# A chain of convolutions and a Haar shrinkage: every matrix product on four 64x64 tiles of the array, images in blocks of 64 rows

## The chip, the cores and the metric

The kernel runs on one core of a Trainium2 chip. Its time is the device time of one execution, in microseconds (us). Each measurement is the median of several executions; the profile comes from one execution of its own. The engines are named as in the profile: PE multiplies matrices (PEld is its loading of weights), DVE is the vector engine, ACT the scalar engine, POOL the general one, and SP issues the DMAs.

## The reference, cut to what matters

The input is `x` with 4 images of 64 channels, 256x256 each, all in float32. Four layers follow each other:

```python
x = conv(x, filters of layer 0)      # L0
x = shrink(x, v, conv_w, tau)        # L1
x = conv(x, filters of layer 2)      # L2
x = conv(x, filters of layer 3)      # L3
```

A convolution layer makes two one-dimensional filters of 256 values for each channel (`hx`, `hy`, small networks of sines), and convolves each image with their product, causally in both directions:

```python
k = jnp.einsum('ijk,imk->ijmk', hx, hy)[0]           # by channel: outer product
y = irfft2(rfft2(x, s=(512, 512)) * rfft2(k, s=(512, 512)) / 512)[..., :256, :256]
out = y + x * bias[:, None, None]
```

The shrinkage layer transforms each image with a two-dimensional Haar transform, and mixes the channels twice:

```python
f1 = haar2d(x)
for i in range(2):
    f4 = jnp.einsum('bchw,oc->bohw', f1 * v[i], conv_w[i])
    acc = acc + jnp.sign(f4) * relu(jnp.abs(f4) - tau[i])
out = haar2d(acc, inverse=True) + x
```

A separable causal convolution is a product with a triangular Toeplitz matrix on each side, so the kernel computes it with matrix products: first one side ("rows"), which also turns the image, then the other ("columns"), which turns it back.

## The kernel before, in words

**Phases.** A round `t` holds two channels of two images, 4 images of 256x256. There are 32 rounds for each of two groups (pairs of batch entries), 64 in all. Phase A does layer 0 and the forward Haar transform, and stores coefficients in DRAM (`coef`). Phase B takes coefficients of all 64 channels, mixes and shrinks them and stores them (`mixed`), in 64 steps of two units for each group. Phase C does the inverse Haar transform and layers 2 and 3, and stores the result.

**Order.** The schedule is written out by hand. Each phase is a list of small pieces; `beside(main, side, ...)` runs a main list and spreads a side list evenly between its pieces. The stages in time are: A for group 0 alone, with the making of the filters beside it; A for group 1 with B for group 0 beside it, called B(0); a short passage from the last of A to the first of C; C for group 0 with B(1) beside it; C for group 1 alone. Each engine works its instructions in the order of the program. `later` keeps back the reading of a PSUM bank until the next piece begins (`flush`).

**Toeplitz products.** `toeplitz` (L282 to L287) is called for each image and each side. An image lies on all 128 partitions, as two blocks of 128 rows. For each of two column blocks it issues a matmul with 256 columns (L286) and one with 128 (L287), since the upper triangle is zero:

```python
nc.tensor.matmul(ps[:, m, :], data[:, 0, cut], t[:, which, :], start=True, stop=False)
nc.tensor.matmul(ps[:, m, HALF:], data[:, 1, cut], t[:, which, :HALF], start=False, stop=True)
```

That is one bank of PSUM per image; four banks (`acps`) rotate. ACT copies the bank of a row product to SBUF (L363 in A, L774 in C); DVE adds `bias` times the old image to that of a column product (L374, L788). `load_toeplitz` (L121) loads the Toeplitz matrices of two channels from DRAM, four DMAs of 128 KB.

**Haar transforms.** One direction is done along the free axis by POOL (`forward_free`, L295/L300, 16 operations in A; `inverse_free`, L321/L323, 16 in C). The other is on PE in several forms: A multiplies with a Haar matrix of 128 (L394, copied out by ACT at L403), or, for half the images of its first 30 rounds, transposes (L412) and lets DVE do the sums (L434 to L464). C multiplies one half and transposes the other (L717, L718), with ACT and DVE putting them together (L727, L724, L725); its last 32 rounds transpose only (L739), with 17 sums on DVE (L750 to L760) for each half of a round. `coarsest` (L467) has three small POOL operations per round.

**Phase B.** One unit multiplies coefficients with weights of `conv_w` (`mix`), multiplies the result by `v` (L579, DVE), takes its sign (L588, ACT) and its magnitude (L591, ACT), subtracts `tau` (L595, DVE), and shrinks (L598, DVE). POOL adds the results (`add`, L603/L606; packed: L617/L620). B(0) is unpacked: rows of 64 channels and two neighbouring image rows lie on the partitions, and a unit is two matmuls of the whole array with 512 columns (L575). B(1) is packed: a unit is four matmuls on 64x64 tiles (L564), whose results lie crossed, so ACT copies half of them to the other half of the partitions (`exchange`, L613). B(0) loads `v` and `tau` (L550) as two rows of 4 KB, repeated for 64 channels; B(1) loads them from copies in DRAM (`v2`, `taus2`), 16 rows with 8 repeats each.

**DMAs.** All are issued by SP in order. A round of A loads `x` (1 MB), and stores its coefficients in one DMA (L479, 1 MB); a round of C loads `g` in one (L695) and stores `out` in one (L797). A step of B loads `ft`, `v` and `tau` and stores `mixed`, 512 KB each.

## Time and profile before

| | us |
|---|---|
| median of 3 executions | 2809.62 (2809.46 to 2810.77) |
| the profiled execution | 2810.75 |
| its span, first to last instruction | 2809.0 |
| busy PE, DVE, POOL, ACT | 2763.1, 1964.7, 1955.6, 1275.8 |
| 384 Toeplitz passes: L286 with L287 in each of the six products of a round | 309 + 197 busy for each of six |
| A alone, about 34 rounds | 24 to 484 |
| A with B(0) | 484 to 1119 |
| the passage | 1119 to 1163 |
| C with B(1), 30 rounds | 1163 to 2015 |
| C alone, 34 rounds | 2015 to 2809 |

The stages are told apart by the first and last instruction of L575 and L564. Busy times of a group are unions: two records of one matmul overlap, and groups overlap each other, so those of L286 and L287 don't add up to PE's. A float32 matmul leaves two records of its own and two weight loads. The granted clock of PE is full (1.00) throughout. 661.91 MB are moved at a mean of 236 GB/s.

### The profile page before, as it was taken

What the parts mean: (1) busy time and instruction counts of PE and PEld (TensorE: products, weight loads), DVE (VectorE), ACT (ScalarE), POOL (GpSimd) and SP (SyncE); (2) the same over time, 40 slices, a digit from 0 to 9 for tenths busy, and PEclk for the clock granted to TensorE, in tenths of its full rate; (3) what the DMA queues carried; (4) which work ended last, traced back from release to release, by engine and by line L of the source; (5) the groups of instructions that cost most, each with busy time, mean ns of one, the idle gap of its engine ahead of it and who ended that gap; (6) DMA issues with size and microseconds to landing.
All of it is one profiled execution on the core that took longest, in us unless ns stands there. A gap on an engine that the chain in (4) does not pass through costs nothing.

```text
span 2809.0 us, 47062 instructions
## 1 busy us (share of the span) xinstructions
PE 2763.1 (98%) x16940; PEld 2343.8 (83%) x16940; DVE 1964.7 (70%) x3461; ACT 1275.8 (45%) x1859; POOL 1955.6 (70%) x2486
## 2 busy tenths in 40 slices
PE   7999999999999999999999999999999999999999
PEld 6989999777777777877777787777899999999998
DVE  3676663888878888378888888888755566666664
ACT  2344443555555555366666666666522222222222
POOL 3777777888888889867777777777764445555540
PEclk9999999999999999999999999999999999999999
DMA  7758886988888887599989989999644444444442
GB/s 205 231 186 263 260 258 248 345 323 320 324 323 320 324 322 277 197 291 287 276 261 267 280 270 277 270 263 281 188 155 144 148 137 139 137 137 135 136 139 80
DMA packets 237447, 661.91 MB, mean 236 GB/s; under 512 B 26622, under 2 KB 135711, under 8 KB 204704
## 3 DMA queue, kind: packets, MB, share of 16 engines
q1 hardware_dynamic: 237216, 658.90, 72.0%
q8 instruction: 136, 2.23, 0.3%
q14 instruction: 95, 0.78, 0.1%
HBM read 438.60 MB, written 220.20 MB: 235 GB/s over the span
## 4 chain that ended last, share of the span: by engine, by line
PE 86%; DVE 5%; issue 3%; POOL 2%; ACT 2%; DMA 1%; SPq 0%; DVEq 0%; ACTq 0%; POOLq 0%
PE c2c L286 8%; PE c1r L286 8%; PE c1c L286 8%; PE c2r L286 8%; PE a1ps L286 6%; PE f L575 6%; PE a2ps L286 6%; PE f L564 5%; PE c2c L287 4%; PE c1c L287 4%; PE c2r L287 4%; PE c1r L287 4%; PE a3ps L394 4%; PE a1ps L287 3%; PE a2ps L287 3%
## 5 line engine op out<-in xcount | busy, mean ns | idle before, releaser
L588 ACT ACTIVATE m<-f 128x1024 f32<-128x1024 f32 x256 | 262.3, 1024 | 495.5 <-DVE f L579 468.2
L595 DVE TENSOR_TENSOR f<-f,tau 128x1024 f32<-128x1024 f32 x256 | 315.0, 1230 | 164.0 <-ACT f L591 163.8
L579 DVE TENSOR_TENSOR f<-f,v 128x1024 f32<-128x1024 f32 x256 | 314.4, 1228 | 57.7 <-PE f L564 38.9
L286 PE MATMUL a1ps<-toep,x 128*128 128x256 f32 x1024 | 308.3, 383 | 3.2 <-DMA toep<-filt 3.2
L598 DVE SCALAR_TENSOR_TENSOR m<-f,m 128x1024 f32<-128x1024 f32 x256 | 311.1, 1215 | 0.0
L286 PE MATMUL c2c<-toep,ch 128*128 128x256 f32 x1024 | 309.2, 384 | 0.0
L286 PE MATMUL c1c<-toep,ch 128*128 128x256 f32 x1024 | 309.1, 384 | 0.0
L286 PE MATMUL c2r<-toep,cy 128*128 128x256 f32 x1024 | 309.1, 384 | 0.0
L286 PE MATMUL a2ps<-toep,ay 128*128 128x256 f32 x1024 | 305.7, 380 | 0.0
L774 ACT COPY ch<-c2r 128x512 f32<-128x512 f32 x256 | 149.4, 586 | 329.0 <-PE c2r L287 328.3
L774 ACT COPY ch<-c1r 128x512 f32<-128x512 f32 x256 | 148.7, 586 | 314.7 <-PE c1r L287 314.2
L617 POOL TENSOR_TENSOR gt<-m,ft 128x1024 f32<-128x1024 f32 x64 | 151.4, 2365 | 180.2 <-DVE m L598 180.1
L575 PE MATMUL f<-ft,mix 128*128 128x512 f32 x512 | 248.4, 608 | 18.4 <-DVE m L598 11.2
L591 ACT ACTIVATE f<-f 128x1024 f32<-128x1024 f32 x256 | 263.0, 1027 | 0.0
L374 DVE SCALAR_TENSOR_TENSOR x<-x,bias_sb,a2ps 128x512 f32<-128x512 f32 x256 | 188.1, 742 | 69.5 <-PE a2ps L287 59.7
L321 POOL TENSOR_TENSOR i<-g 128x8 f32<-128x8 f32 x63 | 13.6, 216 | 320.3 <-DMA g<-mixed 320.2
L788 DVE SCALAR_TENSOR_TENSOR o<-cy,bias_sb,c2c 128x512 f32<-128x512 f32 x256 | 188.6, 742 | 65.7 <-PE c2c L287 58.4
L403 ACT ACTIVATE f<-a3ps,wcol_sb 128x512 f32<-128x512 f32 x196 | 130.7, 686 | 217.8 <-PE a3ps L394 206.6
L321 POOL TENSOR_TENSOR i<-i,g 128x16 f32<-128x16 f32 x378 | 206.1, 545 | 25.9
L287 PEld LDWEIGHTS a1ps<-toep,x 128*128 128x128 f32 x1024 | 195.9, 191 | 27.0
L287 PEld LDWEIGHTS a2ps<-toep,ay 128*128 128x128 f32 x1024 | 194.6, 190 | 26.4
L287 PEld LDWEIGHTS c1c<-toep,ch 128*128 128x128 f32 x1024 | 194.6, 190 | 26.3
(102 smaller groups left out, 6957.2 us busy)
## 6 DMA issues: line engine op xcount, KB each, us to landing
toep<-filt SPq DMA_DIRECT2D x768, 128.0 KB, 4.1
coef<-f SPq DMA_DIRECT2D x64, 1024.0 KB, 4.4
ft<-coef SPq DMA_DIRECT2D x128, 512.0 KB, 7.1
v<-in_v SPq DMA_DIRECT2D x128, 512.0 KB, 8.0
tau<-taus SPq DMA_DIRECT2D x128, 512.0 KB, 7.6
mixed<-gt SPq DMA_DIRECT2D x128, 512.0 KB, 5.4
g<-mixed SPq DMA_DIRECT2D x64, 1024.0 KB, 7.9
x<-in_x SPq DMA_DIRECT2D x63, 1024.0 KB, 8.4
```

Source lines behind the costliest of these rows:

```text
L286: nc.tensor.matmul(ps[:, m, :], data[:, 0, cut], t[:, which, :], start=True, stop=False)
L287: nc.tensor.matmul(ps[:, m, HALF:], data[:, 1, cut], t[:, which, :HALF], start=False, stop=True)
L321: engine.tensor_tensor(even, s, d, ALU.add)
L374: lambda: nc.vector.scalar_tensor_tensor(s["x1"][:, cut], s["x"][:, cut], bias_sb[:, c : c + 1], ps, ALU.mult, ALU.add)
L575: nc.tensor.matmul(un[u]["f4"][:, j, :], mixers[0][:, u % 2, :], f[:, j, :], start=True, stop=True)
L579: nc.vector.tensor_tensor(f4, f4, weights(u, "v"), ALU.mult)
L588: nc.scalar.activation(un[u]["m"], un[u]["f4"], AF.Sign)
L591: nc.scalar.activation(un[u]["f4"], un[u]["f4"], AF.Abs)
L595: nc.vector.tensor_tensor(f4, f4, weights(u, "tau"), ALU.subtract)
L598: nc.vector.scalar_tensor_tensor(un[u]["m"], un[u]["f4"], 0.0, un[u]["m"], ALU.max, ALU.mult)
L774: later(lambda: nc.scalar.copy(y, ps))
L788: later(lambda: nc.vector.scalar_tensor_tensor(o, old, bias_sb[:, at : at + 1], ps, ALU.mult, ALU.add))
```

## The change

All images are kept as four blocks of 64 rows, and two images of a round lie on the lower half of the partitions, two on the upper. Each product is a set of 64x64 matmuls, and each set goes round the four tiles (row half r, column half c) of the array. A Toeplitz product has four row blocks j, each with four accumulating steps of 256, 192, 128 and 64 columns; a call fills one half of a pair of banks for all four images, and the pair is copied out after two calls.

The Haar transform of the second direction is a set of 64x64 matmuls too, in A (`haar`) and in C, for all rounds; transposes and sums on DVE are gone. POOL's forward transform stops at four sums, and `coarsest` makes the rest, in five operations; two of the coarsest combinations are left to phase B, which does them once for its first two steps (`join`, `part`). B is packed for both groups. A's columns, products and stores run one round later each against its rows, and C does the second convolution of a round beside the first of the next. Coefficients lie in DRAM by step, so that a step reads and writes whole runs, and a round stores and loads them in four DMAs. `x` and `out` are laid out in DRAM as the kernel reads and writes them. B(0) is spread over 27.5 rounds of A, which it joins at 34.5; B(1) over 30 of C.

The diff, cut to its core:

```diff
-PERIOD = N + P
-REPEATS = 24
+PERIOD = N + ROW
+REPEATS = 20
...
+    coef = [coefficients(f"coef{g}") for g in range(GROUPS)]
+    mixed = [coefficients(f"mixed{g}") for g in range(GROUPS)]
...
+    def banks(name):
+
+        return [acps.tile([P, 2, N], F32, tag="ps", name=f"{name}_{r}") for r in range(2)]
...
+    def load_toeplitz(l, t):
...
+        tx = ac.tile([P, CI, N], F32, tag="tx", name=f"tx{l}_{t}", bufs=5)
+        ty = ac.tile([P, N], F32, tag="ty", name=f"ty{l}_{t}", bufs=5)
...
+        for e in range(CI):
+            for r in range(2):
+                rows(tx[r * ROW : (r + 1) * ROW, e, :], 0, e)
+        for e in range(CI):
+            rows(ty[e * ROW : (e + 1) * ROW, :], 1, e)
...
-    def toeplitz(ps, data, t, which):
-
-        for m in range(2):
-            cut = bass.ts(m, P)
-            nc.tensor.matmul(ps[:, m, :], data[:, 0, cut], t[:, which, :], start=True, stop=False)
-            nc.tensor.matmul(ps[:, m, HALF:], data[:, 1, cut], t[:, which, :HALF], start=False, stop=True)
+    TILES = [(r, c) for r in range(2) for c in range(2)]
...
+    def toeplitz(ps, data, t, j):
+
+        for k in range(BLOCKS):
+            for r, c in TILES:
+                nc.tensor.matmul(
+                    ps[r][half(c), j % 2, k * ROW :],
+                    data[half(r), c, k, bass.ts(j, ROW)],
+                    t(r, c)[:, : N - k * ROW],
+                    start=k == 0,
+                    stop=k == BLOCKS - 1,
+                    tile_position=(r * ROW, c * ROW),
+                )
+
+    def haar(ps, data, matrix, j):
+
+        for k in range(BLOCKS):
+            for r, c in TILES:
+                nc.tensor.matmul(
+                    ps[r][half(c), j % 2, bass.ts(k, ROW)],
+                    data[half(r), c, k, bass.ts(j, ROW)],
+                    matrix[half(r)],
+                    start=True,
+                    stop=True,
+                    tile_position=(r * ROW, c * ROW),
+                )
...
     def forward_free(src, dst, name):
 
         cur, half = src, HALF
-        while half >= 1:
+        while half >= BLOCKS:
...
+    def all_rows(grp_tile, c0, images):
+
+        parts = images.rearrange("p (s n) k -> p s (n k)", s=2)
+        return [(rows_of(grp_tile, c0 + e, bp), parts[half(e), bp]) for e in range(CI) for bp in range(2)]
...
+        def product(t, bp):
...
+            two = banks(f"a3ps{bp}_{t}")
+            for j in (2 * bp, 2 * bp + 1):
+                haar(two, blocks(s["fw"]), haarH_sb, j)
+            for b, ps in enumerate(two):
+                f = s["f"][:, 4 * bp + 2 * b : 4 * bp + 2 * b + 2]
+                copy = nc.vector.tensor_copy if b and t < ROUNDS else nc.scalar.copy
+                later(lambda f=f, ps=ps, copy=copy: copy(f, ps))
...
+            nc.gpsimd.tensor_tensor(sums, pair[:, :, :, 0], pair[:, :, :, 1], ALU.add)
+            nc.gpsimd.tensor_tensor(diffs, pair[:, :, :, 0], pair[:, :, :, 1], ALU.subtract)
+            nc.gpsimd.tensor_tensor(f[:, :, 0], sums[:, :, 0], sums[:, :, 1], ALU.add)
+            nc.gpsimd.tensor_tensor(f[:, :, 1], sums[:, :, 0], sums[:, :, 1], ALU.subtract)
+            nc.gpsimd.tensor_tensor(f[:, :, 2:4], diffs, diffs, ALU.add)
...
+            for to, f in all_rows(coef[grp], c0, st[t]["f"]):
+                nc.sync.dma_start(to, f)
...
+            if j < BLOCKS:
+                if t < total:
+                    rows(t, j)
+                if t > 1:
+                    run(st[t - 2]["ops"], 3)
+                if j == 1 and t > 2:
+                    coarsest(t - 3)
+            elif j < 2 * BLOCKS:
+                if 0 < t <= total:
+                    columns(t - 1, j - BLOCKS)
+                if j == BLOCKS and t > 2:
+                    store(t - 3)
+            else:
+                if t > 1:
+                    product(t - 2, j - 2 * BLOCKS)
+                if 0 < t <= total:
                     run(st[t - 1]["ops"], 2)
...
+                at = src.offset + s * 4 * W * COPIES
+                flat = bass.AP(src.tensor, at, [[2 * W, 2 * COPIES], [0, C // COPIES], [1, 2 * W]])
...
+        def join():
+
+            a, b, c, d, t, u = four("f")
+            op = nc.vector.tensor_tensor
+            op(t, a, b, ALU.add)
+            op(b, a, b, ALU.subtract)
+            op(u, c, d, ALU.add)
+            op(d, c, d, ALU.subtract)
+            nc.vector.tensor_copy(c, b)
+            op(a, t, u, ALU.add)
+            op(b, t, u, ALU.subtract)
...
+        def part():
+
+            a, b, c, d, t, u = four("g")
+            op = nc.gpsimd.tensor_tensor
+            op(t, a, b, ALU.add)
...
+            if j < BLOCKS:
+                if t < total:
+                    rows(t, 1, j)
+            elif j < 2 * BLOCKS:
+                if t > 0:
+                    rows(t - 1, 2, j - BLOCKS)
+            elif j < 2 * BLOCKS + 2:
+                product(t + 1, j - 2 * BLOCKS)
+            elif j < 3 * BLOCKS + 2:
+                if t < total:
+                    columns(t, 1, j - 2 * BLOCKS - 2)
+            elif t > 0:
+                columns(t - 1, 2, j - 3 * BLOCKS - 2)
...
+    cut_a, cut_c = (ROUNDS + 2) * A_PIECES + BLOCKS + 1, (ROUNDS - 2) * C_PIECES
+    beside(a[:cut_a], rest, 2, 3 * A_PIECES)
...
+    beside(a[cut_a : -2 * A_PIECES], phase_b(0), 2, 0)
...
+    beside(main, phase_b(1), len(c_first) + 2 * BLOCKS + 6, 0)
```

## The prediction

> **What bounds the kernel now.** I read the busy times first, then the stretches between the stages (busy us and instruction count of PE, weight loads, DVE, ACT, POOL; granted clock; DMA share; GB/s).
>
> ```profile
> PE 2763.1 (98%) x16940; PEld 2343.8 (83%) x16940; DVE 1964.7 (70%) x3461; ACT 1275.8 (45%) x1859; POOL 1955.6 (70%) x2486
> ```
>
> ```profile
> 24.00:484.00 460.00, 457.41 (x3025) 426.79 (x3025) 272.82 (x676) 184.45 (x333) 341.85 (x628) 1.00 0.76 240
> 484.00:1119.00 635.00, 616.61 (x3112) 461.58 (x3111) 512.99 (x488) 363.20 (x472) 558.84 (x642) 1.00 0.88 323
> 1119.00:1163.00 44.00, 41.66 (x290) 39.00 (x289) 21.17 (x38) 17.09 (x28) 34.21 (x59) 1.00 0.51 186
> 1163.00:2015.00 852.00, 850.18 (x5497) 680.52 (x5495) 680.13 (x848) 537.80 (x735) 633.98 (x622) 1.00 0.90 269
> 2015.00:2809.00 794.00, 790.21 (x5015) 732.52 (x5008) 467.79 (x1388) 170.71 (x292) 385.79 (x533) 1.00 0.41 134
> ```
>
> The stages are A alone, A with B(0), the passage, C with B(1), C alone. PE is full in all; beside B, POOL and DMA are next. A busy PE need not be PE at its peak, so next the timeline, where starts count and ends are modelled.
>
> ```profile
> 1500.56 0.60 PE L286 MATMUL c2r<-toep,cy 128*128 128x256 f32 x2
> 1500.99 0.38 PE L287 MATMUL c2r<-toep,cy 128*128 128x128 f32 x2
> 1501.21 0.60 PE L286 MATMUL c2r<-toep,cy 128*128 128x256 f32 x2
> ```
>
> A product leaves two records. Two of 256 columns take 0.43 us, two of 128 take 0.22: PE streams without gaps, loads are hidden. The sum: 384 passes (64 rounds x 6) x 8 x 0.655 = 2012 us; unpacked mixing 512 x 0.429 = 220; packed 128 x 1.02 = 131; L394 1568 x 0.112 = 175; transposes and L717 1520 x 0.111 = 168. That is 2706 of 2763 busy.
>
> Then four tiles, where the kernel already uses them (L564):
>
> ```profile
> 1503.93 1.09 PE L564 MATMUL f<-ft,mix 64*64 64x512 f32 x8
> 1504.95 0.70 PE L286 MATMUL c2c<-toep,ch 128*128 128x256 f32 x2
> ```
>
> Four 64x64 products of 512 columns take 1.02 us to the next start; one after another at 0.86 they would take 3.4. The single records start 6.7 ns apart, and the second loads 53 ns after the first, under running matmuls.
>
> Last, the DMA view of A with B(0), then of C with B(1) (KB each, median us to landing):
>
> ```profile
> q1 hardware_dynamic: 60319, 204.42, 87.7%
> ...
> v<-in_v SPq DMA_DIRECT2D x62, 512.0 KB, 7.3
> tau<-taus SPq DMA_DIRECT2D x62, 512.0 KB, 6.5
> ```
>
> ```profile
> q1 hardware_dynamic: 79968, 227.90, 89.7%
> ...
> v<-in_v SPq DMA_DIRECT2D x64, 512.0 KB, 8.6
> tau<-taus SPq DMA_DIRECT2D x64, 512.0 KB, 9.2
> ```
>
> The same bytes land later when packed, at fewer GB/s. With the 4 KB packets assigned in the order of SP's issues, one of v or tau takes 163 ns in the first stage and 290 or 277 in the second; one of ft or mixed 166 to 173 in both.
>
> [...]
>
> **The change part by part.**
>
> *Toeplitz.* A pass of a round had 8 x 384 columns over the whole array; now each of four tiles gets 4 row blocks j x (256+192+128+64) = 2560. At 0.833 ns per column and record (the two pairs' slope) plus 3.75 per record (0.655 us against 0.640), a j takes 2 x 640 x 0.833 + 8 x 3.75 = 1.10 us, a pass 4.39 instead of 5.24. Over 384: 1685 instead of 2012, -327. There is no room below that.
>
> *Haar products.* Both directions now take 16 matmuls of 64 columns per tile and round: 4 x (8 x 57 ns) = 1.83 us, 234 in all. L394, transposes and L717 (343) go: -109. The loads are the doubt: one of 128 columns takes 108 ns start to start, one of 64 about 53, just what its matmul streams. If they don't overlap a record costs some 80: +95 us in all.
>
> *Mixing.* All 256 units packed[...]: 0.87 us each (0.85 to 1.02), 223 instead of 351, -128. PE's total: 2142, 564 less.
>
> *Issue.* Matmuls go from 8,974 to 33,806, PE's instructions to some 135,000: 16.7 ns each in Toeplitz, 6.7 in Haar. Between semaphore records of PE around eight loads and matmuls of L575 lie 74 ns at least: 9 each or less. I take issue as hidden by streaming; the other end is in the rivals. PE's instruction packets (2.23 MB, about 1.0 us each, one per 256 instructions, fetched with about 256 in hand) get 4.3 us each, in Haar 1.7: 0 to 60 us, I take 0.
>
> *POOL.* L295/L300 lose the last four of 16 operations, `coarsest` has five for three: 2 x (1.89+1.04+0.62+0.41+0.30+0.25) + 5 x 0.22 = 10.1 us per round of A. The inverse stays at 11.7, B's additions at 4.73 per step: some 2000 in all, unchanged.
>
> *DVE and ACT.* DVE's transforms go (L434 to L464, L724 to L760: 578 us of means); copies of banks come (128 on DVE, 384 on ACT, some 586 ns each), ACT's exchange doubles to 256 x 1.04. DVE 1.61 ms, ACT 1.47, both beside PE or DMA. `join` puts seven DVE operations before B's first mix and `part` eight on POOL before two stores: at L724's and L321's rates 5 and 10 us, twice. PE has A or C to do meanwhile; without that cover 30 us.
>
> *DMAs.* Filters fall from 512 to 384 KB per load, in six pieces for four; coefficients are stored and loaded in four of 256 KB for one of 1 MB. B(0) now loads v and tau packed, as B(1) did: its step goes from 128 x 663 to 128 x 903 ns. A round of A with B(0), over 16 engines: filters 384 x 61, x 128 x 328, coef 256 x 168, 2.33 steps x 128 x 903: 23.6 us (19.2 before). C with B(1): 768 x 60 + 256 x 170 + 128 x 370 + 2.17 x 128 x 903: 24.2 (25.4 before). The same sums gave 0.86 and 0.895 for the stages before, measured 0.88 and 0.90. SP issues 2413 for 1649, each behind the one eight before it (a wait in the build's order): a late landing or store holds filters, x, v, tau, g behind it; PE waits for filters, POOL for g. Both are asked for half a round ahead or more: nothing charged but the slack below.
>
> *PSUM.* A pair of banks fills in 2.2 us, and the other must be copied out meanwhile: 1.2 us on ACT, 1.5 on DVE. Free alone; with B's operations of 1.2 us queued ahead it is 0 to 3 us a round.
>
> **By stage.** A alone, 34.5 rounds: PE 10.6, POOL 10.1, tied by a loop: residual 1.9, POOL 10.1, then PE's product, rows and columns 10.6, in two periods: 11.3 each, 390 us (460). A with B(0), 27.5 rounds: PE 15, POOL 21.1, DVE 20, DMA 23.6; DMA bounds, and at 96% full (single 25 us stretches of before reach 100%) 24.5: 674 (635). Start and passage 24 + 42, as before. C with B(1), 30 rounds: PE 19.4 + 4.35 x 0.87 = 23.2, POOL 22.0, DVE 21.9, ACT 20.5, DMA 24.2; five nearly full in fixed order I put at 26 (24.5 to 28.4), less 9 that its first round lacks: 771 (852). C alone, 34 rounds and that half: 34 x 19.7 + 9 = 678 (794). Sum 2579 against the span of 2809.0. Its execution took 2810.75, 1.1 above the median of 2809.62; median less span is 0.6: 2580.
>
> **Rivals.**
> - *Coupling eats more.* C with B stays at 28.4 a round, A with B at 25.5: 2580 + 72 + 27 = 2679. For: PSUM slack 2.2 us, B's fixed order. Against: PE ran A with B at 97% with POOL at 88 and DMA at 88.
> - *v and tau land unhindered.* If their 283 ns came from C's traffic, not from the pattern, A with B follows POOL: 22 a round, C with B 25: 2580 - 69 - 30 = 2481.
> - [...]
> - *Slower: loads share that floor.* [...] It decides from 26 ns a pair, where my sum passes 2810. For: the trace has no more than eight pairs in a row, and a queue could hide a slow issuer. Against: those 74 ns.
> - *Tiles don't run side by side when accumulating.* Each pass quadruples; L564 speaks against it. Counted with the last.
>
> **Chances.** Likeliest (2500 to 2650) 0.52; coupling 0.11; unhindered 0.13; one floor 0.08; slower 0.15; no change to be told 0.01. The range 2460 to 2750 takes in the first three. Within 0.2% (5.6 us) is about what a measurement can't tell from no change.
>
> **What would show it.** Right: a j of Toeplitz starts 1.10 us after the last; Haar matmuls of one tile follow at 57 ns; DMA is over 0.95 in A with B(0); C alone takes under 20 us a round. Wrong: [...] "issue" ahead of loads; PE in C with B waiting on DVE or ACT for its banks.

## The result, and the profile after

The changed kernel takes 3067.02 us (median of 4 executions, 3059.91 to 3076.29) against 2809.7 us (2809.46 to 2810.77): a ratio of 1.0917, with a 95% interval of 1.0882 to 1.0952. It is 9% slower, where 8% faster was forecast. The profiled execution took 3059.91 us, its span is 3058.1.

The busy times of the page of the changed kernel (busy us, share, instructions):

```profile
PE 2461.0 (80%) x67612; PEld 2159.1 (71%) x67612; DVE 1564.4 (51%) x1765; ACT 1370.3 (45%) x1927; POOL 1942.9 (64%) x2358
```

PE lost its bound as forecast: 80% instead of 98%. DVE, ACT and POOL came out near the 1.61, 1.47 and 2.0 ms forecast. Yet over the whole span nothing else is full either, so something idles all of them. The stretches of the changed kernel, stage by stage (busy us and instructions of PE, weight loads, DVE, ACT, POOL; granted clock; DMA share; GB/s):

```profile
23.00:541.00 518.00, 418.14 (x13140) 382.89 (x13144) 167.94 (x237) 116.52 (x211) 330.87 (x573) 0.96 0.74 203
541.00:1238.00 697.00, 501.96 (x11036) 379.32 (x11032) 508.85 (x483) 477.24 (x586) 545.26 (x562) 0.89 0.94 280
1238.00:1348.00 110.00, 62.28 (x1964) 55.48 (x1960) 36.27 (x64) 29.71 (x51) 66.20 (x116) 0.83 0.66 177
1348.00:2256.00 908.00, 753.91 (x19072) 653.33 (x19076) 591.62 (x603) 546.71 (x716) 615.25 (x573) 0.95 0.84 234
2256.00:3058.00 802.00, 718.04 (x22406) 685.16 (x22396) 250.01 (x353) 197.61 (x361) 384.42 (x530) 0.98 0.48 129
```

The stages here end at the first and last mixing matmul of each B. By this the passage of the kernel before is 75 us and its C with B(1) 821; the forecast counted 44 and 852, so the two are taken together below. The last two columns of the table are experiments that come further down.

| stage, us | before | forecast | after | e3: 61,000 PE instructions | e12: and other DMA forms |
|---|---|---|---|---|---|
| start | 24 | 24 | 23 | 23 | 25 |
| A alone | 460 | 390 | 518 | 465 | 419 |
| A with B(0) | 635 | 674 | 697 | 689 | 665 |
| passage, C with B(1) | 896 | 813 | 1018 | 958 | 858 |
| C alone | 794 | 678 | 802 | 688 | 686 |
| span | 2809 | 2579 | 3058 | 2823 | 2653 |

The place to read first is C alone: there DMA is at 0.48, POOL at 48%, and the clock is nearly full, so the 124 us above the forecast should be PE's own. PE's timeline in it, in a stretch without trouble (start, us, and how many records follow each other):

```profile
2600.91 4.36 PE L308 MATMUL c2c<-ty,ch 64*64 64x256 f32 x121
...
2605.27 4.36 PE L308 MATMUL c1r<-tx,z 64*64 64x256 f32 x121
```

A pass takes 4.36 us from one to the next; 4.39 was forecast. The Haar products stream as forecast too, when they stream:

```profile
2402.21 1.10 PE L719 MATMUL c0ps<-haarW_sb,ci 64*64 64x64 f32 x62
```

Less the last record's 0.22 that is 14.4 ns from start to start, 58 for each of four tiles, where 57 was forecast. But a Haar stretch two rounds later looks so:

```profile
2449.69 1.95 PE L719 MATMUL c0ps<-haarW_sb,ci 64*64 64x64 f32 x94
2454.03 1.02 PE L719 MATMUL c0ps<-haarW_sb,ci 64*64 64x64 f32 x27 [2.39 <-issue]
```

PE stands still for 2.4 us in the middle of a run of equal matmuls, and "issue" says that it waited for no semaphore and no other engine. The waits of PE in C alone (us in total, times, longest) are all of this kind:

```profile
PE c0ps L719 <- issue: 47.7, 31, 2.7
PE c1c L308 <- issue: 14.6, 18, 1.5
PE c2r L308 <- issue: 10.8, 11, 1.8
```

What it waited for is in the queue that brings PE's instructions (packets, MB, share of 16 engines):

```profile
q8 instruction: 532, 8.72, 1.2%
```

That is 16 KB a packet, and 532 packets for PE's 136,000 instructions make 256 instructions a packet; the kernel before had 136 packets. Laid over PE's records, the packets explain the stalls. I counted PE's instructions in the trace from the start and subtracted 256 for each packet that had come. In C alone, up to 3050 us, two starts on PE lie over 0.5 us apart 63 times. In 31 of these stalls a packet ends, and these 31 stand at one place; a few of them, from the records:

```
stall from   long   place in the stream   packet began   took   PE went on after its end
2307.62      2.15   449                   0.42 before    1.21   1.36
2380.04      2.53   449                   0.08 before    1.26   1.35
2451.42      2.61   449                   0.01 after     1.25   1.34
2786.08      2.68   449                   0.01 before    1.35   1.34
```

The number 449 itself only says where the count began; that it is the same in all says that each stall begins exactly where the instructions in hand end. In another 31 the packet had ended at most 1.0 us before, so the count stands 256 lower, at 193: the same point. So 62 of the 63 stalls, 91 us, begin there, and PE goes on 1.2 to 1.7 us after the end of the packet. A packet begins 0 to 3.8 us (median 1.2) after PE has begun its last 256, takes some 1.1, and is usable some 1.4 later: 3.6 us in the median, 6.5 at most, which the 256 in hand have to cover. They last 4.36 us in Toeplitz, and 1.83 in Haar. In the kernel before, 256 instructions lasted 19.5 us in the median, and no such stall is in its trace.

DMA was as forecast in A with B(0), and fell beside C (packets, MB, share of 16 engines), the first:

```profile
q1 hardware_dynamic: 59968, 193.89, 92.8%
```

and C with B(1):

```profile
q1 hardware_dynamic: 75808, 209.72, 83.0%
```

### The profile page after: what moved, and what is told of

Its sections match the earlier page's. It is cut to its first block, busy times and chain, and to the rows that moved or that the text cites. A ratio compares the mean times of both kernels' runs of the same rounds, so it can differ in the third digit from the quotient of the medians.

```text
span 3058.1 us, 147507 instructions
## 1 busy us (share of the span) xinstructions
PE 2461.0 (80%) x67612; PEld 2159.1 (71%) x67612; DVE 1564.4 (51%) x1765; ACT 1370.3 (45%) x1927; POOL 1942.9 (64%) x2358
## 4 chain that ended last, share of the span: by engine, by line
PE 45%; issue 11%; ACT 10%; DMA 8%; DVE 6%; POOL 4%; SPq 2%; ACTq 0%; DVEq 0%; POOLq 0%
PE c1c L308 10%; PE c2c L308 9%; PE c1r L308 9%; PE c2r L308 7%; PE f L584 4%; DVE f L595 3%; PE c0ps L719 3%; DMA v<-in_v 3%; ACT m L601 3%; ACT f L604 2%; ACT other L617 2%; ACT ch L742 2%; PE a1ps L308 2%; DMA ft<-coef 2%; PE a2ps L308 2%
## 5 line engine op out<-in xcount | busy, mean ns | idle before, releaser
L584 PE MATMUL f<-ft,mix 64*64 64x512 f32 x2048 | 337.7, 668 | 181.2 <-DVE m L611 82.1
L308 PEld LDWEIGHTS a1ps<-tx,x 64*64 64x64 f32 x8192 | 327.7, 143 | 148.1 <-issue 86.3
L308 PE MATMUL a1ps<-tx,x 64*64 64x128 f32 (+3 forms) x8192 | 360.9, 317 | 83.5 <-issue 46.6
L308 PE MATMUL c1c<-ty,ch 64*64 64x256 f32 (+3 forms) x8192 | 339.9, 309 | 45.4 <-issue 40.5
L308 PEld LDWEIGHTS c1c<-ty,ch 64*64 64x64 f32 x8192 | 312.6, 139 | 82.2 <-issue 56.3
L308 PE MATMUL c2c<-ty,ch 64*64 64x64 f32 (+3 forms) x8192 | 326.8, 304 | 49.2 <-issue 49.0
L308 PE MATMUL a2ps<-ty,ay 64*64 64x256 f32 (+3 forms) x8192 | 330.4, 303 | 32.4 <-issue 28.2
L308 PE MATMUL c1r<-tx,z 64*64 64x256 f32 (+3 forms) x8192 | 326.2, 304 | 31.6 <-issue 31.6
L308 PEld LDWEIGHTS c1r<-tx,z 64*64 64x64 f32 x8192 | 308.5, 137 | 60.2 <-issue 43.6
L308 PE MATMUL c2r<-tx,cy 64*64 64x256 f32 (+3 forms) x8192 | 320.4, 299 | 29.9 <-issue 29.4
```

The source lines that it names most:

```text
L308: nc.tensor.matmul(ps[r][half(c), j % 2, k * ROW :], data[half(r), c, k, bass.ts(j, ROW)], t(r, c)[:, : N - k * ROW], start=k == 0, stop=k ...
L584: nc.tensor.matmul(un[u]["f4"][half(to), i, :], mixers[0][half(q), bass.ts(i, C)], f[half(q), u % 2], start=True, stop=True, tile_position ...
```

## The experiments

Theory A was that PE's instruction fetch holds the changed kernel. Rivals were that a short product with its load costs more by itself, and that the half clock after idle stretches does it: the trace of the changed kernel has 75 stretches at 0.50 of full speed, 347 us in all, and before 74 of them PE stood idle for 27 to 73% (median 42%) of the 6.8 us ahead. Where a kernel is compared by stages, they are those of the table above. e1 to e7 edit the changed kernel.

**e1: one Haar matmul of 256 columns for four of 64.** 111,000 PE instructions for 135,000.

```diff
-        for k in range(BLOCKS):
-            for r, c in TILES:
...
-                    ps[r][half(c), j % 2, bass.ts(k, ROW)],
-                    data[half(r), c, k, bass.ts(j, ROW)],
-                    matrix[half(r)],
+        for r, c in TILES:
...
+                ps[r][half(c), j % 2, :].rearrange("p (k q) -> p k q", k=BLOCKS),
+                data[half(r), c, j, bass.ts(j, ROW)],
+                matrix[half(r)].unsqueeze(1).to_broadcast([ROW, BLOCKS, ROW]),
```

> The Haar products of both directions issue one step of 256 columns (the 64 columns of the matrix read four times) instead of four steps of 64, so three of four row blocks are left out of them; columns and their time stay, and PE's instructions fall from 135,000 to 111,000. Theory A (PE runs out of fetched instructions in the Haar stretch, where 256 instructions are worked in 1.8 us and a packet takes over 3.3): the stalls of 1.1 to 2.9 us in each Haar stretch go, C alone falls from 22.2 to about 20 us a round, A alone from 14.9 to about 13, in all about 2900. Rival B (the gaps are waits for PSUM banks, DVE or ACT, or plain load of DMA): nothing in those waits changes, 3040 to 3070. Rival C (the half clock makes the difference by itself): half-clock time stays near 347 us and the time near 3060.

Measured: 2888.15 us, ratio to the kernel before 1.0277 [1.0207, 1.0347]. A alone 474, A with B(0) 690, C with B(1) 874, C alone 724. Theory A holds, and the half clock is out: its sum is 336 us, for 347 in the changed kernel, while the time fell by 179.

**e2: Toeplitz steps of 512 and 128 columns for four of 256 to 64.** 86,000 instructions, the same columns.

```diff
-        for k in range(BLOCKS):
-            for r, c in TILES:
...
+        for r, c in TILES:
...
+                t(r, c).unsqueeze(1).to_broadcast([ROW, 2, N]),
...
+        for r, c in TILES:
...
+                t(r, c)[:, : 2 * ROW],
```

> Each Toeplitz step set of 256, 192, 128 and 64 columns becomes one of 512 and one of 128: the same 640 columns in half the instructions (the second, third and fourth block are read wrongly or left out). PE's instructions fall to 86,000. Theory A: 256 instructions now last 8.6 us in a pass, so the buffer is full when a Haar stretch begins, and both kinds of stalls go: 2580 to 2750. Rival B: 3040 to 3070, since columns, banks and copies stay. Rival C: as B unless the half clock goes by itself.

Measured: 2881.09, 1.0252 [1.0201, 1.0303]. The direction is theory A's, the size is not: C alone is still 739, A 471, and the whole misses theory A's 2580 to 2750. Haar still uses up 256 instructions in 1.83 us, and C with B(1), at 849, has a second cause.

**e3: both.** 61,000 instructions.

> Both edits: the columns of the whole program stay, PE's instructions fall from 135,000 to 61,000 (parts of both products are left out or read wrongly). Theory A: the time of the sum that the prediction made without fetch, 2530 to 2640, with C alone at 19.5 to 20 us a round and A with B(0) still held by DMA near 24.5. Rival B: above 3000.

Measured: 2822.48, 1.0041 [1.0021, 1.0061]. C alone went where the forecast had it, 688 for 678, and PE is full in it:

```profile
2135.00:2823.00 688.00, 680.34 (x10120) 508.12 (x10112) 249.83 (x353) 197.24 (x363) 386.01 (x532) 1.00 0.58 152
```

So the forecast for four tiles was right there to 10 us, and fetch was most of its error: no stall at the end of the instructions in hand is left in e3, where they made 92 us of C alone. A pass of e3 is also 0.05 us shorter (4.31), some 7 us in 34 rounds of four. But A alone (465), and the passage with C and B(1) (958), stayed 75 and 145 over it, and the whole missed theory A's 2530 to 2640: theory A alone doesn't make up the loss.

**e6: Toeplitz steps of 64 columns only, all 135,000 instructions.** A pass streams 1024 columns per tile for 2560.

```diff
-                    ps[r][half(c), j % 2, k * ROW :],
+                    ps[r][half(c), j % 2, bass.ts(k, ROW)],
...
-                    t(r, c)[:, : N - k * ROW],
+                    t(r, c)[:, :ROW],
```

> The opposite: every Toeplitz step gets 64 columns (most of the product is left out), instructions stay at 135,000, columns per pass fall from 2560 to 1024. Without a bound on instructions a pass would take 1.83 us instead of 4.36 and C alone would be held by POOL and DVE, near 13 us a round. Theory A: packets of 256 instructions need 3.3 to 4 us each, five of them a round: C alone 16.5 to 20 us a round, in all 2500 to 2800. Rival B: PE's work falls by 960 us, so 2100 to 2300, bound by DMA and POOL.

Measured: 3057.55, 1.088 [1.0799, 1.096]. With 60% of the Toeplitz columns gone A alone is 518 as before the edit, and C alone 782 for 802. There PE's time is set by the number of its instructions, not by what they stream. Theory A's range, 2500 to 2800, was still missed: in C alone a packet comes every 4.4 us (176 in 781 us), not every 3.3 to 4. The granted clock fell, to 0.87 in C alone, but does not explain it: five stretches of 1.83 us a round at half that speed (0.50) throughout make 622 us in 34 rounds, an estimate from these figures.

**e7: the two halves of a Haar product put apart**, with Toeplitz between, nothing left out.

```diff
+                if j == BLOCKS + 1 and t > 1:
+                    product(t - 2, 0)
...
-                    product(t - 2, j - 2 * BLOCKS)
+                if t > 1 and j == 2 * BLOCKS + 1:
+                    product(t - 2, 1)
...
-                product(t + 1, j - 2 * BLOCKS)
+                if j == 2 * BLOCKS:
+                    product(t + 1, 0)
...
+                if j == 3 * BLOCKS + 1:
+                    product(t + 1, 1)
```

> The changed kernel with nothing left out: only the order of PE's work differs. The two halves of each Haar product, which stood next to each other (256 PE instructions that stream in 1.83 us), are put apart: in A the first half comes after the second j of columns, in C the second half comes after the first columns pass, so that 128 instructions of Haar (0.92 us) always have at least 2.2 us of Toeplitz between them. The instruction count stays at 135,000. Theory A (PE's instruction fetch gives 256 instructions per 3.3 us at best, and Haar, which uses 256 in 1.83 us, drains it): the stalls shrink without an instruction less; A alone from 518 to some 470, C with B(1) from 908 to some 860, C alone from 802 to some 700; in all 2850 (2800 to 2920). Rival B (each 64-column product with its load costs more than 57 ns by itself, wherever it stands): nothing changes, 3040 to 3080. Rival C (each packet costs PE a stall of its own, however evenly it is used): the number of packets is the same, so 3040 to 3080 too.

Measured: 3122.55, 1.1121 [1.1086, 1.1156]. C alone is 803 for 802. My version of theory A, a rate of one packet per 3.3 us that only has to be kept on average, falls: it is a delay of 3.6 us in the median and 6.5 at most that 256 instructions have to cover, and halves with 2.2 us of Toeplitz between them leave stretches of 256 that last 3.1. An unchanged C alone is also what both rivals of this run had. Against the first stands the stream of 58 ns for each tile above; against the second, a stall with every packet, stands e3, whose packets come without one. In A the edit cost 55 us for a reason of its own: the earlier product waits for POOL (69 us of waits for `fw` where the changed kernel has 2).

*The second cause.* What is left in e3 I looked for in the DMAs. The waits of e3 in C with B(1):

```profile
POOL i L377 <- DMA g<-mixed: 172.4, 26, 9.8
PEld f L591 <- issue: 70.3, 19, 5.9
PE f L591 <- DMA ft<-coef: 67.4, 21, 5.7
```

and those of its SP:

```profile
SPq L147 <- DMA ft<-coef: 82.2, 42, 3.4
SPq L147 <- DMA v<-in_v: 62.6, 42, 2.9
SPq L147 <- DMA tau<-taus: 51.4, 44, 2.0
```

SP, about to load filters, waits for earlier transfers to land: each issue waits on the one eight before it (in the trace of the kernel before none of the 820 issues of which it tells this began before the one eight before had landed). 716 issues in 851 us, with 8.06 us to landing where the trace tells it, make 6.8 of 8 in flight; the kernel before had 534 issues in 821 us at 6.70, 4.4 in flight. In A alone SP is at its issues for most of the time: 480 issues take 350 us, and the short pauses between them 27, of 465.

**e8: two issues for each set of filters**, on e3.

```diff
-        for e in range(CI):
-            for r in range(2):
-                rows(tx[r * ROW : (r + 1) * ROW, e, :], 0, e)
-        for e in range(CI):
-            rows(ty[e * ROW : (e + 1) * ROW, :], 1, e)
+        rows(tx, 0, [[4, P], [REPEATS * PERIOD, CI]])
+        rows(ty, 1, [[REPEATS * PERIOD, CI], [4, ROW]])
```

> Base is the kernel with merged Haar and merged Toeplitz products (2822 us; A alone 465, C with B(1) 851, C alone 688). Each set of filter loads (6 issues on SP, 1 KB packets) becomes 2 issues with the same packets and bytes, by a plain step of 4 elements from row to row; it leaves out the Toeplitz shift, so values differ. SP has 480 issues in A alone, 350 us of issue and 27 between them in 465. Theory S (SP's issues bound A alone): 336 issues, A alone falls to 395-420, C with B(1) to some 820, C alone stays at 680-690; in all 2700 to 2760. Rival T (A alone is held by the loop through POOL, DVE and PE, or by clock and DMA): A alone stays at 455 to 470, in all 2800 to 2830.

Measured: 2812.55, 1.0008 [1.0002, 1.0015]. A alone fell to 431, part of the way to theory S's 395 to 420, but A with B(0) and C with B(1) rose to 701 and 865. The load of `ty` has an outermost step of 2 here; with 128 in its place (e16) the kernel takes 141 us less.

**e16: the same with 128 rows outermost** in `ty` too.

```diff
-        rows(ty, 1, [[REPEATS * PERIOD, CI], [4, ROW]])
+        rows(ty, 1, [[4, P]])
```

> Base is again the kernel with merged products (2822 us). Only the filters change: six issues become two, each with 128 rows in its outer step (it leaves out the Toeplitz shift). The earlier form with two issues had an outer step of 2 in one of them and gave A 431, C with B(1) 865. Theory F (SP's 0.6 us for each of six issues holds A, and C with B(1) as well): A 425-435, C with B(1) 800-825; in all 2730 to 2770. Theory K (the filters count in A alone): A 425-435, C with B(1) 840-855; in all 2780 to 2800.

Measured: 2671.24, 0.9498 [0.9482, 0.9513]: 151 us less than e3. A alone 425, A with B(0) 670, C with B(1) 762. Theory F holds beyond its range: the number of issues held C with B(1) too. Each transfer now goes to 128 partitions in place of 64, but the packets take as long as before: in C with B(1) 67 ns for 1 KB and 235 for 4 KB, in e3 69 and 236. POOL's wait for `g` there falls from 172 us to 2, and the DMA share rises from 0.88 to 0.98. So it is the issues, and not the time of the packets.

**e15: one issue of 1 MB for a round's coefficients** in place of four of 256 KB for 64 partitions each, still in 4 KB packets; on e3.

```diff
-        return [(rows_of(grp_tile, c0 + e, bp), parts[half(e), bp]) for e in range(CI) for bp in range(2)]
+        rows = bass.AP(grp_tile.tensor, grp_tile.offset + c0 // 2 * n, [[C * n, P], [C // 2 * n, CI], [1, n]])
+        return [(rows, images.rearrange("p (s n) k -> p s (n k)", s=2))]
```

> Base is the kernel with merged products (2822 us; A 465, A with B(0) 689, passage 108, C with B(1) 851, C 688). Only the coefficients change: the four stores or loads of 256 KB for 64 partitions each become one of 1 MB for 128 partitions, still in 4 KB packets (it leaves out which row and channel goes where). With this, two issues for each set of filters, and 8 KB packets together, C with B(1) was 759. Theory W (a transfer to 64 partitions has the slow packets, 293 ns for g): g at 165 to 200 ns, C with B(1) 780-810, A with B(0) 670-680; in all 2710 to 2760. Theory K (the length of the packets or the filters made it): g stays near 290, C with B(1) 820-850; in all 2780 to 2820.

Measured: 2722.73, 0.9695 [0.9672, 0.9718]: 100 us less than e3. In C alone, where 4 KB packets are almost only `g`, one takes 168 ns on the mean for 272 in e3. Theory W holds for the packets: those of the transfers to half of the partitions are slow. The medians are 307 ns in e3 and 159 here; what makes them slow was not shown. But the edit also makes one issue of four. How much of the 100 us the packets are worth is not told apart here; e16 gains more with the packets of `g` as slow as before (276 ns).

**e12: both, with 8 KB packets for coefficients.**

```diff
+        rows(tx, 0, [[4, P], [REPEATS * PERIOD, CI]])
+        rows(ty, 1, [[4, P]])
...
+        rows = bass.AP(grp_tile.tensor, grp_tile.offset + c0 * n, [[C * n, P], [1, CI * n]])
```

> Base is the kernel with merged products (2822 us). Two parts of the DMA side go back to the form of the kernel before, with the same bytes: the six filter loads of a set become two (rows 4 elements apart, 128 rows each; it leaves out the Toeplitz shift), and the four stores or loads of a round's coefficients, 256 KB in 4 KB packets for 64 partitions each, become one of 1 MB in 8 KB packets for all 128 (it leaves out which row goes to which partition). SP's issues fall from 2413 to some 1260. With two issues for each set of filters alone A fell from 465 to 431 and C with B(1) did not. Theory S (SP's issues and the slower coefficient packets, 205 and 293 ns against about 165, hold the passage and C with B(1)): A alone 395-415, A with B(0) 665-690, passage 85-95, C with B(1) 790-825, C alone 675-688; in all 2640 to 2740. Rival T (these are held by the packets of v and tau and by waits of B's chain): only A gains a little more, in all 2780 to 2815.

Measured: 2658.28, 0.9467 [0.9451, 0.9483], within theory S's range for the whole, with C with B(1) better (759) and the passage worse (99). Its stretches of A alone and of C with B(1):

```profile
25.00:444.00 419.00, 390.90 (x5524) 264.28 (x5526) 169.34 (x237) 116.32 (x211) 330.29 (x573) 0.98 0.74 246
...
1208.00:1967.00 759.00, 712.48 (x9148) 494.62 (x9148) 584.66 (x603) 539.97 (x715) 614.19 (x573) 0.98 0.91 279
```

PE is at 93 and 94%. The gains of e15 and e16 overlap: 164 together for 100 and 151, so on top of e16 the form of the coefficients is worth only 13.

**e9 and e13: the order of rows in the loads of `v` and `tau`**, on e3. e9:

```diff
-                flat = bass.AP(src.tensor, at, [[2 * W, 2 * COPIES], [0, C // COPIES], [1, 2 * W]])
+                flat = bass.AP(src.tensor, at, [[0, C // COPIES], [2 * W, 2 * COPIES], [1, 2 * W]])
```

> Base is again the kernel with merged products (2822 us; A with B(0) 689, C with B(1) 851). The load of v and tau takes 16 rows of 4 KB, each for 8 partitions in succession; here the same 16 rows are taken in turn, 16 after each other, eight times over, so the bytes, packets and issues are equal and only the order of rows differs. It leaves out that each half of the partitions gets its own row, so values differ. Theory D (the packed pattern of v and tau is what slows those packets, 283 against 163 ns, and these bound A with B(0)): 2.33 steps of 256 packets each less 120 ns over 16 engines, 4.5 us per round of A with B(0); A with B(0) from 689 to 590-640, C with B(1) from 851 to 800-830; in all 2690 to 2750. Rival E (the packets are slow from the other traffic, or POOL bounds at 21 to 24 us): A with B(0) at 675 to 690, in all 2800 to 2825.

Measured: 3168.12, 1.1269 [1.125, 1.1287], A with B(0) 833 at a DMA share of 0.80. Neither theory foresaw that. The outermost step fell from 16 to 8. In this run as in e8, with a step of 2, the time rises while DMA's share falls, here from 0.94 to 0.80 in A with B(0), and in C with B(1) from 0.98 in e16 to 0.90 in e8; why it falls was not shown. e13 keeps 16 steps:

```diff
+                flat = bass.AP(src.tensor, at, [[0, 2 * C // COPIES], [2 * W, COPIES], [1, 2 * W]])
```

> Base is the kernel with merged products (2822 us; A with B(0) 689, C with B(1) 851). The loads of v and tau keep their packets, bytes, issues and 16 outer steps, but each outer step now takes eight rows in turn where it took one row eight times (it leaves out which half of the partitions gets which row, so values differ). The earlier order with 8 outer steps changed both at once: DMA's share fell and the time rose, so it told nothing on the rows. Theory D (the same row eight times in succession is what makes a packet take 283 ns in place of 163): v and tau at 160 to 190 ns, A with B(0) 600-640, C with B(1) 800-830; in all 2700 to 2770. Rival E (packets are slow because all of the traffic is): 250 to 290 ns as before, in all 2800 to 2830.

Measured: 2819.3, 1.0039 [1.0025, 1.0053], packets of `v` and `tau` at 290 and 246 ns. Theory D falls: repeating one row is not what makes them slow.

**e14: e12 with e13's rows.**

> All at once: merged Haar and Toeplitz products (61,000 PE instructions), two issues for each set of filters, one for a round's coefficients, and eight rows in turn for v and tau; it leaves out what each of these leaves out. If the instruction fetch, SP's issues, the coefficient packets and the repeated rows are together what the prediction left out, the stages should meet or pass its forecast (390, 674, 42, 771, 678): A alone 395-415, A with B(0) 590-640, passage 80-95, C with B(1) 750-790, C alone 675-688; in all 2530 to 2620. If there is another cause (the half clock after idle stretches, the chain of B through PE, DVE and ACT), A with B(0) and C with B(1) stay over 660 and 810, in all 2660 to 2750.

Measured: 2660.39, 0.9466 [0.9452, 0.9481], the same as e12: the repeated rows are no part of what is left, and another cause remains.

**e11: the kernel before with B(0) packed**, one part of the change alone.

```diff
-    beside(a[cut_a : -6 * M], phase_b(0, False), 5 * M, 0, [13] * (2 * M) + [9] * M)
+    beside(a[cut_a : -6 * M], phase_b(0, True), 5 * M, 0, [13] * (2 * M) + [9] * M)
```

> One part of the change alone, in the kernel before: B(0) runs packed (v and tau for two halves, mixing on four tiles), as B(1) did already; all else is the kernel before. Theory D (the packed loads of v and tau make A with B(0) bound by DMA): 27.5 rounds go from 23.1 us to 24 or more, A with B(0) from 635 to 665-690, the rest unchanged: 2840 to 2865. Rival E (PE sets A with B(0) at 97% busy, and packed mixing takes from PE 128 units of about 0.7 us): A with B(0) falls by 30 to 90 to 550-605, in all 2720 to 2780.

Measured: 2846.65, 1.0124 [1.0108, 1.014]. A with B(0) is 668 for 635, all else nearly as before: packing as a whole, its loads and its mixing, costs 33 us, near what the forecast had for this stage (674).

**e17: e12's DMA forms in the changed kernel**, all 135,000 instructions.

> The changed kernel with all of its 135,000 PE instructions, and the DMA forms of the 2658-us run (two issues for each set of filters, one 1 MB transfer of 8 KB packets for a round's coefficients; it leaves out the Toeplitz shift and which row goes to which partition). If the two causes add up, it gains the 164 us that these forms gained with merged products: 2900 (2880 to 2925). If they cover each other (PE starved of instructions in A and C, whatever the DMAs do): A stays at 500 or more, C with B(1) over 880, C alone 795-802; in all 2960 to 3020.

Measured: 3017.55, 1.0735 [1.0685, 1.0786]. 50 us, not 164: A alone is 532, C alone 796, C with B(1) 873. The first cause covers most of the second. A line of the changed kernel shows it, against 172.4 in e3, in C with B(1):

```profile
POOL i L370 <- DMA g<-mixed: 4.0, 2, 2.8
```

PE is so late that `g` is there in time.

**e18: coefficients in memory by channel**, nothing left out: one issue per round in A and C, two of 64 partitions per step in B.

```diff
+        rows = bass.AP(grp_tile.tensor, grp_tile.offset + c0 * ROW * n, [[n, P], [C * ROW * n, 2], [1, n]])
...
+            for q in range(2):
+                nc.sync.dma_start(d["f"][half(q)].rearrange("p b w -> p (b w)"), step_of(coef[grp], s, q))
```

> The changed kernel with nothing left out: the coefficients lie in memory by half of the steps, channel and row, so that a round's coefficients are stored or loaded in one issue of 1 MB with 4 KB packets for 128 partitions in place of four, and B's step is loaded and stored in two issues of 64 rows in place of one. SP's issues: 384 fewer in A and C, 256 more in B. If it is the number of SP's issues in A and C and the form for 64 partitions: A 500-510, passage 95-105, C with B(1) 850-880; in all 2990 to 3030. If B's two transfers to 64 partitions are as slow as A's four were: A with B(0) and C with B(1) rise or stay, in all 3050 to 3110.

Measured: 3106.57, 1.1056 [1.1038, 1.1074]. What A saves (511) B pays: A with B(0) 741. It moves the transfers to half of the partitions, and doesn't remove them. In C alone, where `g` now goes to all partitions, its 4 KB packets take 179 ns, for 273 in the changed kernel.

**e19: columns of two images on 64x128 tiles**, nothing left out; 111,000 instructions.

```diff
+        for k in range(BLOCKS):
+            for r in range(2):
+                nc.tensor.matmul(
+                    ps[r][:, j % 2, k * ROW :],
+                    data[half(r), k, j].rearrange("p c q -> p (c q)"),
+                    t(r, 0)[:, : N - k * ROW],
...
+                    tile_position=(r * ROW, 0),
```

> The changed kernel with nothing left out and fewer PE instructions: in the second pass of a convolution both images of a half meet the same filter, so one load and one matmul of 64x128 take the two side by side (the copy out of PSUM lays them next to each other), and a pass has 128 PE instructions for 256, in the same 4.4 us. In all some 111,000 for 135,000. Theory A (instructions are fetched too slowly for it): A alone 470-490, C with B(1) 860-880, C alone 715-735; in all 2880 to 2930, as with the merged Haar products at 111,000 (2888). Rival ([...] two tiles side by side are not as fast as four): 3040 to 3150.

Measured: 3024.75, 1.0772 [1.0754, 1.079]: better than the changed kernel by 42 us, short of the 2880 to 2930. A alone is 501, C with B(1) 878, but C alone 815. Its timeline there:

```profile
2600.30 4.98 PE L325 MATMUL c2c<-ty,ch 64*128 64x256 f32 x64
2605.21 4.59 PE L308 MATMUL c1r<-tx,z 64*64 64x256 f32 x128
```

A pass on 64x128 tiles takes 4.9 us for 4.36. Each of its four row blocks takes 1.20 us for 1.09, and the change to 64x64 after them some 0.1 more. So the rival is right that two tiles are slower than four; the change of tiles costs little, those 0.1 us.

**e20: e19 with e12's DMA forms.**

> The same 111,000 PE instructions with the DMA forms of the 2658-us run (two issues for each set of filters, one 1 MB transfer for a round's coefficients; it leaves out the Toeplitz shift and which row goes to which partition). With all 135,000 instructions these forms gained 50 us, with 61,000 they gained 164. If fetch and DMA cover each other as far as PE is starved, the gain lies between: A 430-460, C with B(1) 800-830, C alone 715-730; in all 2770 to 2840. If the forms only count once PE is not starved at all: 2840 to 2890.

Measured: 3005.32, 1.0693 [1.0667, 1.0718]: outside both. The forms gain 20 us here, less than with more instructions, and C alone is 841; there the stalls at the end of the instructions in hand make 92 us, in e19 70. Why they grew I can't say.

No version that leaves nothing out beats the kernel before.

## Why the prediction was wrong

Step by step, as the prediction put them:

- *Toeplitz, Haar, mixing as streams.* Right: 4.36 us a pass for 4.39, 58 ns for 57; C alone in e3 is 688 for 678.
- *Issue.* This is the step that failed. "PE's instruction packets (2.23 MB, about 1.0 us each, one per 256 instructions, fetched with about 256 in hand) get 4.3 us each, in Haar 1.7: 0 to 60 us, I take 0." The 1.0 us is only the packet's own transfer (1.1 here). With what passes before it begins and until PE goes on it is 3.6 us in the median and up to 6.5. The term was some 235 us: the span of the changed kernel less that of e3. The stalls of over 0.3 us at the end of the instructions in hand add up to more, 79, 21, 7, 166 and 92 us in A alone, A with B(0), the passage, C with B(1) and C alone; e3 has none. Beside B a part of them cost nothing, since DMA would have held the stage: A with B(0) is only 8 us longer than in e3. The count of instructions was right in the prediction (135,000), and so was the number in hand; both stood beside a stream of 1.83 us for 256 (by its own sums a packet had 4.39 and 1.83 us, not 4.3 and 1.7).
- *DMAs, by time.* Right for A with B(0): forecast 674 and DMA at 0.96, measured 697 at 0.94, and 665 at 0.97 in e12; e11 shows what packing alone adds. Wrong for the coefficients: "coef 256 x 168" and "256 x 170" took the packets of 128 partitions for those of 64; they take 205 and 293 ns.
- *DMAs, by issue.* Wrong: "Both are asked for half a round ahead or more: nothing charged but the slack below." Once PE is no longer starved, six filter issues for two cost 151 us (e16), and with the coefficient transfers 164 (e12). It was not the time of the packets (e16). How much of it is the time of an issue on SP, and how much the limit of eight in flight, was not told apart.
- *PSUM, POOL, DVE, ACT.* Near enough; none sets a stage.
- *The loop of A*, 11.3 us a round: not reached in any run; e12 has 12.1. C with B(1) and the passage are 45 us over in e12. What holds these 74 us is open; the clock after idle stretches (0.81 in the passage, 0.92 in A with B(0) in e12) and B's chain were not tried by themselves.

The rivals: the slower one was the nearest. It had loads and matmuls share one feed and decide "from 26 ns a pair". Packets came at least 3.24 us apart in C alone, 25 ns a pair; but the feed is the fetch and not the issue, and it bites in short stretches, so that the whole came out 257 us over the kernel before. Its argument against itself, eight pairs in 74 ns, spoke of instructions already in hand. I gave it 0.15. Coupling, "unhindered" (e13 and the packets' 290 ns are against it) and the one floor under the matmuls of all tiles (over four tiles records start 14.4 ns apart, and the measurement decides) did not come.

So the loss has two causes. The fetch is shown by e1, e2, e3, e6 and by the place of the stalls; SP's many issues are shown by e16. Transfers to 64 partitions have slow packets (e15, e18), but what these cost in time is not shown by itself. In the changed kernel most of the second cause hides behind the first (e17). Either alone is enough to miss the 2580: without the fetch e3 takes 2822, with few issues e17 takes 3018. Open is what delays a packet's beginning by 0 to 3.8 us.

## What to carry to other kernels

Before a matmul is cut into smaller ones, divide the length of the shortest stretch of 256 PE instructions by the full delay of a fetch, from the room for it to the first instruction that uses it (here 3.6 us in the median and 6.5 at most), and not by the transfer of the packet (1.1); in this kernel 8.6 us was enough (two passes of e3, 4.31 each), and 4.4 was not (at 2399.8 us the changed kernel stalls for 1.67 behind 256 instructions of Toeplitz that lasted 4.49). Smaller tiles also cut the transfers: count the issues per round against the number that may be in flight (eight here), and look at what each transfer costs in its form: 4 KB packets took 272 ns to 64 partitions and 168 to 128 (e3 and e15), and 8 outermost steps in place of 16 cost 346 us (e9). Here two issues in place of six for each set of filters were worth 151 us, once the fetch no longer hid them. After a large loss is removed, look again at each stage: a cause that was covered can be as large as the first.

## What was not expected of the hardware

- PE's instructions come with 256 in hand, and 62 of the 63 stalls in C alone began exactly at the end of these, to end 1.2 to 1.7 us after a packet of 0.9 to 1.4 us.
- The 4 KB packets of a transfer to 64 partitions take 272 ns where those to 128 take 168 (e3 and e15, C alone); the first come as four transfers for one.
- The same 128 KB with 2 outermost rows in place of 128 cost 141 us in the whole kernel (e8 and e16); 8 for 16 in `v` and `tau` cost 346 (e9 and e3).
- With the packed pattern `v` and `tau` stay at 250 to 290 ns a packet, whether a row is repeated or not (e13); why is open.
- Two 64x128 tiles take 4.9 us for what four 64x64 tiles do in 4.36.
